# Ordering the last stage of a four-layer graph network by a planned list over pairs of super-tiles, with q k in seven products, and reordering loads and preparations of the graph part

## The chip, the cores and the metric

The kernel runs on one core of a Trainium2 chip. The metric is the device time of one execution in microseconds (us). Engines are named as in the profile: PE is TensorE (matrix products and transposes), DVE is VectorE, ACT is ScalarE, POOL is GpSimd, SP is SyncE, which here only issues DMAs. Each engine works through its own queue in program order; an instruction that waits for another engine holds up everything behind it in its queue.

## The reference, cut to what matters

The input x is 128 graphs of 64 nodes with 256 features (8192 rows in float32); adj is one 64 x 64 matrix for all graphs. Four layers follow one another, each of the form x = x + layer(relu(layernorm(x))):

```python
# layer 0: two graph convolutions, then four LSTMs over windows of 1..4 nodes
h = relu(einsum('ts,bsh->bth', adj, h @ Wg0 + bg0))
h = relu(einsum('ts,bsh->bth', adj, h @ Wg1 + bg1))
# layer 1: graph product, 256 -> 512 -> 256, batchnorm after each product
# layer 2: diagonal, upper and lower part of adj, each with its own weights
h = einsum('bjf,kfo->kbjo', x, W)
out = adj_0 h[0] + adj_1 h[1] + adj_2 h[2] + bias
# layer 3: causal attention inside each graph, adj added to the scores
q, k, v = split(x @ Wqkv, 3)
scores = where(causal, einsum('btd,bsd->bts', q, k) * scale + adj_mask, NEG)
y = einsum('bts,bsd->btd', softmax(scores), v) @ Wo
```

## The kernel before

The 8192 rows are cut into 16 super-tiles of 512 rows, each four tiles of 128 rows (q = 0 to 3, two graphs in each); the 256 features are two halves of 128 (c = 0, 1). Everything is float32. The program has five parts: the graph part (the two convolutions), the LSTM part, the first product of layer 1, its second product, and the last stage with layers 2 and 3. PSUM has 8 banks that `bank()` hands out in turn, so a bank is used again eight requests later.

**How the order is set.** The order of the instructions on every engine is the order in which the program makes them; no scheduler moves them. In most parts the program first fills a list `events` with `at(t, fn, ...)`, where t is a planned time, sorts it by t and calls the functions. The planned times set nothing but the order. A "round" of the graph part is 10 planned us, one super-tile in each of its steps.

**Graph part (lines 288 to 475).** `load` (L298) brings x of a super-tile by one DMA (four for the first); `stats`, `root`, `shift` and `relu` make the layernorm: bn_stats and bn_aggr on DVE, an add on DVE and the power -1/2 on POOL (L316), a small product on DVE (L319), the relu on ACT (L323). PE multiplies with adj (`aggregate0`, L331) and with Wg0 (`weigh`, L341), DVE adds the row sums of adj times the bias (L347), ACT makes the relu (L352). The product with Wg1 (L370) has the seven-product form of a 2 x 2 block product: POOL makes sums of blocks (`sums`, L362), PE adds seven 128 x 256 products into three banks a, b and c, and DVE reads a bank between two products that are added into it (`begun`, L377, and `add`, L384). The last super-tile takes the direct form (L391). Among the rounds stand preparations for later parts: `adjacencies` (L139, DVE), `degrees_root` (L154, POOL), `degrees`, `normalize` (L176) and sums of the first LSTM weights (`weight_sum`, L275, POOL). Wg0 is loaded from ACT's queue (L104).

**Second product (L795 to L881).** The list form with seven products; at its end come the batchnorm coefficients co2 (L881), then transposes of Wqkv (L890) and the weight product Wq Wk^T into wqk (L897, L899).

**Last stage (L904 to L1010).** `rest(s)` is a generator for one super-tile, and `pipelined(..., 2)` starts one every second step and lets each live one take one step in turn, the youngest first. The steps are: load x1 and affine of the batchnorm on DVE (L912); transposes back to rows (L227) and add (L228); layernorm (L191 to L195, L201), then the bias bl2 added on POOL as one 128 x 1024 operation (L922); products with the three parts of adj, 64 rows at a time (L933), copied to `ag` half by ACT and half by DVE (L938); the product with the three weights (L946) and add (L948), layernorm; transposes (L957, L958); q k as eight direct 128 x 512 passes (L964) copied by ACT (L966), and the values times Wv Wo (L972, L974); scores (L980), mask and maximum (L983, L986), exponentials with their sums on ACT (L988); transposes of these (L993, L995); the product with the values (L1001), the division and the sum (L1004), and the store.

Of the kernel before, what the change touches and what calls it, by code (L numbers as in the profile page):

```python
# [20 lines left out]
def kernel(ctx: ExitStack, tc: tile.TileContext, a: dict, out: bass.AP):  # L21
# [82 lines left out]
    wg0 = weight("wg0", a["Wg0"], first, nc.scalar)  # L104
# [34 lines left out]
    def adjacencies():  # L139

        nc.vector.tensor_add(lbias, con["bih"], con["bhh"])


        scr = first.tile([P, P], F32, tag="scr", name="scr")
        nc.vector.tensor_add(scr, adj_bd, ident)
        nc.vector.reduce_sum(deg[:, 0:1], scr, axis=AX.X)
        nc.vector.tensor_mul(scr, scr, ident)
        nc.vector.reduce_sum(deg[:, 1:2], scr, axis=AX.X)
        nc.vector.tensor_add(ahT, adjT_bd, ident)
        nc.vector.reduce_sum(deg[:, 2:3], ahT, axis=AX.X)  # L150
        nc.vector.tensor_add(deg[:, 0:1], deg[:, 0:1], deg[:, 2:3])
        nc.vector.tensor_sub(deg[:, 0:1], deg[:, 0:1], deg[:, 1:2])
# [136 lines left out]
    with tc.tile_pool(name="pa", bufs=2) as pa, tc.tile_pool(name="pax", bufs=3) as pax:  # L289
        events, wih0, made = [], [], []  # L290

        def graph_part(s):
# [5 lines left out]
            def load():  # L298
                v["xt"] = pax.tile([P, Q, D], F32, tag="xt", name="xt")
                for part in ([slice(q, q + 1) for q in range(Q)] if s == 0 else [slice(0, Q)]):  # L300
                    nc.sync.dma_start(v["xt"][:, part, :], x_r[s, :, part, :])
# [35 lines left out]
            def weigh(k):  # L337
                p_ = v["W", k] = bank().rearrange("p (q d) -> p q d", q=2)
                for q in range(2):
                    for c in range(KC):  # L340
                        nc.tensor.matmul(p_[:, q, :], v["g0"][:, c, ts(2 * k + q, P)], wg0[:, c, :],  # L341
# [62 lines left out]
            if s == 0:  # L404
                halves = ((slice(0, 2), -8.6), (slice(2, 4), -7.4))
# [30 lines left out]
            for k in range(4):  # L436
                at(late + 7.2 + 0.7 * k, sums, k)
# [21 lines left out]
            if s == 4:  # L459
                at(5.0, adjacencies)  # L460
                at(11.5, degrees_root)
                at(13.3, lambda: made.append(degrees()))
            if s == 5:
                at(0, lambda: wih0.append(load_lstm(a["WihT"][0], "wih", lwa)))
            if s == 7:
                at(0.4, lambda: normalize(made[0]))
            if s == 9:
                for k in range(4):
                    at(0.4 + 2.5 * k, lambda k=k: weight_sum(wih0[0], k))
# [298 lines left out]
    with tc.tile_pool(name="pz", bufs=1, reuse_waits="tile") as pz:  # L768
# [19 lines left out]
        wqk = late.tile([P, KC, D], F32, tag="wqk", name="wqk")  # L788
        wvo = late.tile([P, KC, D], F32, tag="wvo", name="wvo")
# [111 lines left out]
        weight_product(0, wT[:, KC : 2 * KC, :], wqk)  # L901


    with tc.tile_pool(name="pc", bufs=2, reuse_waits="tile") as pc, \  # L904
            tc.tile_pool(name="pc1", bufs=1, reuse_waits="tile") as pc1:

        def rest(s):
            x1 = pc.tile([P, Q, D], F32, tag="x1", name="x1")
            nc.sync.dma_start(x1, x1d[s])
            y = [yslot(s, c) for c in range(KC)]  # L910
            for c in range(KC):
                nc.vector.tensor_scalar(y[c], y[c], co2[:, 0, c : c + 1], co2[:, 1, c : c + 1],  # L912
                                        op0=ALU.mult, op1=ALU.add)
            yield
            x2 = pc.tile([P, Q, D], F32, tag="x2", name="x2")
            to_token_major(lambda c, q: y[c][:, ts(q, P)], x1, x2)
            if s == 0:
                weight_product(2, wo, wvo)


            h = layernorm_relu(pc, x2)
            nc.gpsimd.tensor_add(x2, x2, bcast_q(bl2))  # L922
            yield
            ag = pc1.tile([P, KC, 3, SUP], F32, tag="ag3", name="ag3")

            for c in range(KC):
                for q2 in range(0, Q, 2):
                    half = [bank()[:, : 6 * T].rearrange("p (q k n) -> p q k n", q=2, k=3)
                            for _ in range(2)]
                    for q in range(2):  # L930
                        for b in range(2):
                            r = slice(b * T, (b + 1) * T)
                            nc.tensor.matmul(half[b][:, q], h[r, q2 + q, ts(c, P)], adj3[r, :, r],  # L933
                                             start=True, stop=True)
                    for b in range(2):
                        copy = nc.vector.tensor_copy if b else nc.scalar.copy
                        to = ag[:, c, :, q2 * P : (q2 + 2) * P].rearrange("p k (q n) -> p q k n", q=2)
                        copy(to[:, :, :, b * T : (b + 1) * T], half[b])  # L938
            yield
            x3 = pc.tile([P, Q, D], F32, tag="x3", name="x3", bufs=4)  # L940
            for q2 in range(0, Q, 2):
                p_ = bank().rearrange("p (q d) -> p q d", q=2)
                for q in range(2):
                    for n in range(3 * KC):
                        c, k = divmod(n, 3)
                        nc.tensor.matmul(p_[:, q, :], ag[:, c, k, ts(q2 + q, P)], wl2[k][:, c, :],  # L946
                                         start=(n == 0), stop=(n == 3 * KC - 1))
                nc.vector.tensor_add(x3[:, q2 : q2 + 2, :], x2[:, q2 : q2 + 2, :], p_)  # L948


            h = layernorm_relu(pc, x3, "ln_h3")
            yield
            h3T = pc.tile([P, KC, SUP], F32, tag="h3T", name="h3T")
            for c in range(KC):
                p_ = bank()
                for q in range(Q):
                    nc.tensor.transpose(p_[:, ts(q, P)], h[:, q, ts(c, P)], ident)  # L957
                nc.vector.tensor_copy(h3T[:, c, :], p_)  # L958
            yield
            qk = pc1.tile([P, KC, SUP], F32, tag="qk", name="qk")  # L960
            for o in range(KC):
                p_ = bank()
                for c in range(KC):
                    nc.tensor.matmul(p_, wqk[:, c, ts(o, P)], h3T[:, c, :],  # L964
                                     start=(c == 0), stop=(c == KC - 1))
                nc.scalar.copy(qk[:, o, :], p_)  # L966
            hw = pc.tile([P, Q, D], F32, tag="hw", name="hw")
            for q2 in range(0, Q, 2):
                p_ = bank().rearrange("p (q d) -> p q d", q=2)
                for q in range(2):  # L970
                    for c in range(KC):
                        nc.tensor.matmul(p_[:, q, :], h3T[:, c, ts(q2 + q, P)], wvo[:, c, :],  # L972
                                         start=(c == 0), stop=(c == KC - 1))
                nc.scalar.copy(hw[:, q2 : q2 + 2, :], p_)  # L974
            yield

            p_ = bank()
            for q in range(Q):
                for c in range(KC):
                    nc.tensor.matmul(p_[:, ts(q, P)], qk[:, c, ts(q, P)], h3T[:, c, ts(q, P)],  # L980
                                     start=(c == 0), stop=(c == KC - 1))
            sc = pc1.tile([P, Q, P], F32, tag="sc", name="sc")
            nc.vector.scalar_tensor_tensor(sc, p_.rearrange("p (q n) -> p q n", q=Q), D ** -0.5,  # L983
                                           bcast_q(smask), op0=ALU.mult, op1=ALU.add)
            mx = pc.tile([P, 3, Q], F32, tag="mx", name="mx", bufs=3)
            nc.vector.tensor_reduce(mx[:, 0, :], sc, AX.X, ALU.max, negate=True)  # L986
            for q in range(Q):
# [61 lines left out]
```

## Time and profile before

| what | value |
|---|---|
| median of 3 runs (lowest, highest) | 1912.3 us (1910.62, 1914.24) |
| the profiled execution | 1910.58 us, its span 1908.7 us |
| busy share of PE, DVE, ACT, POOL | 98%, 57%, 46%, 31% |
| graph part | up to about 181 us |
| LSTM part, first and second product | up to 1470 us |
| last stage | 1470 to 1908.7 us |
| last stage, share of L946 (PE) in the chain of waits from 1400 us on | 32.6% |

The span is the time from the first to the last recorded instruction of the profiled execution; the difference to its time lies around it. In the chain of waits each piece has a start, a length, and the engine and line that the end of the program waited for in that piece. PE records two passes for one product in float32 (x8 for four products). In a line on waits the first number is the total, the second the count and the third the longest. In a timeline each line has the start, the length, the engine, the line of the kernel, the operation with its result and operands, and in brackets how long the engine had been idle and what released it.

### The profile page before, as it was taken

The page shows a single profiled execution, that of the slowest core. Times are in us where ns is not written, and L with a number is a line of the kernel's source. Part 1 is how long each engine was busy: PE and PEld are TensorE (multiplying, and loading weights), DVE is VectorE, ACT ScalarE, POOL GpSimd, SP SyncE. Part 2 cuts the span into 40 slices and gives each one's busy share as a digit, 9 for nine tenths or more (in the row PEclk, how much of TensorE's full clock was granted, in tenths as well). Part 3 has the DMA queues.
Part 4 walks back from the last instruction along what each step waited for, and adds up shares of the span by engine and source line. Part 5 has one row for each costly group of instructions (what it writes and reads, how often), then busy time and mean ns, then how long its engine had stood idle before and what let it go on. Part 6 is the DMA issues. An engine that isn't in the chain of part 4 may idle for free.

```text
span 1908.7 us, 19347 instructions
## 1 busy us (share of the span) xinstructions
PE 1874.8 (98%) x7022; PEld 1160.6 (61%) x7022; DVE 1092.3 (57%) x2155; ACT 882.2 (46%) x1509; POOL 598.9 (31%) x434
## 2 busy tenths in 40 slices
PE   7999999999999999999999999999999899999998
PEld 7897444444445666665444444555444788888886
DVE  6775777635446345445633334688786555565554
ACT  6676666534435335434533333444574333333332
POOL 4341412543325433331522224533152211111110
PEclk9999999999999999999999999999999999999999
DMA  4110001000001000000000001233100001111111
GB/s 138 56 56 1 1 1 32 13 1 0 1 0 44 1 0 1 1 0 23 0 0 1 1 0 44 77 111 111 64 1 30 26 23 45 45 45 34 33 34 45
DMA packets 49471, 54.31 MB, mean 28 GB/s; under 512 B 3040, under 2 KB 44768, under 8 KB 49376
## 3 DMA queue, kind: packets, MB, share of 16 engines
q1 hardware_dynamic: 48640, 52.61, 8.8%
q8 instruction: 56, 0.92, 0.2%
q10 hardware_dynamic: 736, 0.46, 0.1%
q14 instruction: 39, 0.32, 0.1%
HBM read 36.28 MB, written 16.78 MB: 28 GB/s over the span
## 4 chain that ended last, share of the span: by engine, by line
PE 94%; DVE 3%; ACT 1%; POOL 1%; issue 1%; DMA 0%; SPq 0%; DVEq 0%; ACTq 0%; POOLq 0%
PE ps L599 34%; PE ps L605 19%; PE ps L946 9%; PE ps L515 6%; PE ps L834 5%; PE ps L972 3%; PE ps L964 3%; PE ps L331 3%; PE ps L341 2%; PE ps L933 2%; PE ps L370 2%; PE ps L980 1%; PE ps L217 1%; PE ps L1001 1%; PE ps L227 1%; PE ps L957 1%
## 5 line engine op out<-in xcount | busy, mean ns | idle before, releaser
L621 DVE TENSOR_TENSOR gate<-gate,ps 128x512 f32<-128x512 f32 (+2 forms) x378 | 223.9, 619 | 446.2 <-PE ps L605 366.9
L599 PE MATMUL ps<-tx,wih 128*128 128x512 f32 (+2 forms) x1008 | 446.8, 542 | 2.7 <-ACT gate L624 1.0
L599 PE MATMUL ps<-hT,wih 128*128 128x512 f32 (+2 forms) x756 | 338.5, 541 | 0.0
L624 ACT COPY gate<-ps 128x512 f32<-128x512 f32 (+2 forms) x252 | 134.5, 534 | 378.2 <-PE ps L605 325.1
L599 PEld LDWEIGHTS ps<-tx,wih 128*128 128x128 f32 x1008 | 190.5, 190 | 193.0 <-issue 130.8
L617 ACT ACTIVATE gate<-gate,lbias 128x512 f32<-128x512 f32 (+2 forms) x252 | 216.7, 860 | 157.8 <-DVE gate L621 157.8
L605 PE MATMUL ps<-h,whh 128*128 128x512 f32 (+2 forms) x576 | 256.6, 527 | 0.0
L599 PEld LDWEIGHTS ps<-hT,wih 128*128 128x128 f32 x756 | 143.6, 190 | 141.6 <-issue 79.6
L605 PE MATMUL ps<-th,whh 128*128 128x512 f32 (+2 forms) x432 | 192.4, 527 | 0.0
L194 POOL TENSOR_TENSOR ln_rn<-ln_rn,mhalf 128x4 f32<-128x4 f32 x48 | 48.6, 1012 | 389.1 <-DVE ln_rn L193 389.1
L605 PEld LDWEIGHTS ps<-h,whh 128*128 128x128 f32 x576 | 109.4, 190 | 100.2 <-issue 76.5
L946 PE MATMUL ps<-wl,ag 128*128 128x256 f32 x768 | 168.4, 379 | 0.0
L644 POOL TENSOR_TENSOR gate<-gate 128x1024 f32<-128x1024 f32 (+2 forms) x36 | 71.9, 2017 | 304.7 <-ACT gate L617 304.7
L201 ACT ACTIVATE ln_h<-x,ln_rn 128x256 f32<-128x256 f32 x128 | 66.5, 589 | 199.1 <-DVE ln_rn L195 199.1
L946 PEld LDWEIGHTS ps<-wl,ag 128*128 128x128 f32 x768 | 144.8, 190 | 19.1
L644 POOL TENSOR_TENSOR cell<-gate 128x1024 f32<-128x1024 f32 (+2 forms) x36 | 79.4, 2226 | 175.2 <-ACT gate L617 175.2
L605 PEld LDWEIGHTS ps<-th,whh 128*128 128x128 f32 x432 | 82.1, 190 | 75.2 <-issue 57.4
L515 PE MATMUL ps<-ag,w 128*128 128x512 f32 x256 | 112.3, 592 | 0.0
L644 POOL TENSOR_TENSOR cell<-gate,cell 128x1024 f32<-128x1024 f32 (+2 forms) x32 | 65.1, 2052 | 109.3 <-ACT gate L617 109.3
L624 DVE COPY gate<-ps 128x512 f32<-128x512 f32 (+2 forms) x126 | 78.5, 623 | 20.9 <-PE ps L605 20.9
L649 ACT ACTIVATE gate<-cell 128x1024 f32<-128x1024 f32 (+2 forms) x72 | 68.1, 951 | 29.5 <-POOL cell L644 29.5
L617 ACT ACTIVATE gate<-ps,lbias 128x512 f32<-128x512 f32 (+2 forms) x126 | 79.6, 631 | 3.9 <-PE ps L605 1.0
(199 smaller groups left out, 2693.4 us busy)
## 6 DMA issues: line engine op xcount, KB each, us to landing
xt<-in_x_dram SPq DMA_DIRECT2D x31, 512.0 KB, 4.6
x1d<-xt SPq DMA_DIRECT2D x16, 512.0 KB, 3.0
x<-x1d SPq DMA_DIRECT2D x16, 512.0 KB, 4.4
out_dram<-x SPq DMA_DIRECT2D x16, 512.0 KB, 3.2
wih<-in_WihT_dram SPq DMA_DIRECT2D x16, 256.0 KB, 4.5
whh<-in_WhhT_dram SPq DMA_DIRECT2D x12, 256.0 KB, 5.1
wl<-in_W_dram SPq DMA_DIRECT2D x3, 256.0 KB, 2.9
wqkv<-in_Wqkv_dram SPq DMA_DIRECT2D x1, 768.0 KB, 6.2
```

Source lines behind the costliest of these rows:

```text
L201: nc.scalar.activation(h[:, q, :], src[:, q, :], AF.Relu, bias=rn[:, 1, q : q + 1], scale=rn[:, 0, q : q + 1])
L331: nc.tensor.matmul(p_[:, ts(q, P)], v[h][:, q, ts(c, P)], adjT_bd, start=True, stop=True)
L515: nc.tensor.matmul(p_, con["w1"][:, c, ts(o, P)], ag[:, c, :], start=(c == 0), stop=(c == KC - 1))
L599: nc.tensor.matmul(wide(p_[:, :N]), wih[0][:, OF[k], gi, :], x_, start=first_, stop=(j == 0), skip_group_check=True)
L605: nc.tensor.matmul(p_[:, :N], whh[0][:, OF[k], gi, :], h_, start=False, stop=True, skip_group_check=True)
L617: nc.scalar.activation(to, r[bank_][:, :N] if bank_ else to, fn, bias=lbias[:, l, m : m + 1])
L621: nc.vector.tensor_add(slot(n, hc), slot(n, hc), r[bank_][:, :N])
L624: op(slot(n, hc), r[bank_][:, :N])
L644: fn(*((t["G"] if isinstance(t, dict) and "G" in t else st["c"])[:, n, :, : st["N"]] for t in tiles))
L649: nc.scalar.activation(o_, c, AF.Tanh)
L834: nc.tensor.matmul(banks[name], w2[:, OF[j], k, :], x_, start=(new and k == 0), stop=(k == 1), skip_group_check=True)
L946: nc.tensor.matmul(p_[:, q, :], ag[:, c, k, ts(q2 + q, P)], wl2[k][:, c, :], start=(n == 0), stop=(n == 3 * KC - 1))
```

## The change

**Last stage.** The generator and its turns are gone. `rest(s, at, ...)` now fills one list for all super-tiles, with planned times given per pair of super-tiles (an even and the next odd one), 52.5 planned us from pair to pair, and special times for the first and last pair. Each step of before becomes one or more functions. New in what is computed: q k of 15 super-tiles in seven products with 128 x 256 blocks (`qsum` on DVE, `qproduct`, `qcopy` on ACT, `qadd` on DVE), the last one direct (`qdirect`); the sums of weight blocks for it, `aqk`, are made on POOL from wqk (four copies, four sums) right after the weight product; the bias is added in four 128 x 256 pieces (`biased`); the first super-tile's layernorm is made in two halves; x2 has three buffers and ag two. In the last super-tile exps are turned, and results stored, in halves.

**Graph part.** Wg0 is loaded on SP's queue behind x of the first super-tile; x of the second super-tile comes in four DMAs, not one; the root of the first half-layernorm comes earlier; `sums` 2 and 3 move ahead of the power (8.1) on POOL; `adjacencies` is cut into four pieces in four rounds, with the steps that need it three rounds later; `normalize` moves to round 9; the sums of the first LSTM weights stand 1.6 instead of 2.5 planned us apart.

The diff, cut:

```diff
-    wg0 = weight("wg0", a["Wg0"], first, nc.scalar)
...
-                for part in ([slice(q, q + 1) for q in range(Q)] if s == 0 else [slice(0, Q)]):
+                for part in ([slice(q, q + 1) for q in range(Q)] if s < 2 else [slice(0, Q)]):
...
+                at(-20, lambda: con.update(wg0=weight("wg0", a["Wg0"], first)))
+            if s == 0:
-                halves = ((slice(0, 2), -8.6), (slice(2, 4), -7.4))
+                halves = ((slice(0, 2), -9.1), (slice(2, 4), -7.4))
...
-                at(late + 7.2 + 0.7 * k, sums, k)
+                at(late + (7.2, 7.9, 8.0, 8.05)[k], sums, k)
...
-                at(5.0, adjacencies)
-                at(11.5, degrees_root)
-                at(13.3, lambda: made.append(degrees()))
+                pieces = adjacencies()
+                for k in range(4):
+                    at(5.0 + ROUND * k, next, pieces, None)
+                at(11.5 + ROUND * 3, degrees_root)
+                at(13.3 + ROUND * 3, lambda: made.append(degrees()))
...
-            if s == 7:
-                at(0.4, lambda: normalize(made[0]))
+            if s == 9:
+                at(5.0, lambda: normalize(made[0]))
             if s == 9:
                 for k in range(4):
-                    at(0.4 + 2.5 * k, lambda k=k: weight_sum(wih0[0], k))
+                    at(0.6 + 1.6 * k, lambda k=k: weight_sum(wih0[0], k))
...
         weight_product(0, wT[:, KC : 2 * KC, :], wqk)
+        for o in range(2):
+            for c in range(2):
+                nc.gpsimd.tensor_copy(aqk[:, 2 * o + c, :], wqk[:, c, ts(o, P)])
+        weight_sums(aqk)
+    PERIOD, HALF = 52.5, SUP // 2
...
+        def rest(s, at, only_pair, t_T, t_n, t_G, t_W, t_h, t_QH, t_S, t_soft, t_E, t_O, end):
...
+            def biased(q):
+                nc.gpsimd.tensor_add(v["x2"][:, q, :], v["x2"][:, q, :], bl2)
...
+            def qsum(k):
+                if k == 1:
+                    v["t"] = pc1.tile([P, 5, HALF], F32, tag="tq", name="tq")
+                t = v["t"]
+                nc.vector.tensor_sub(t[:, k], *(None, (b_(0, 1), b_(0, 0)), (b_(1, 1), t[:, 1]),
+                                                (b_(1, 1), b_(0, 1)), (b_(1, 0), t[:, 2]))[k])
...
+                nc.tensor.matmul(v["q", name], aqk[:, OF[j], :], x_, start=new,
+                                 stop=(name, j) in (("a", 4), ("b", 3), ("c", 2)), skip_group_check=True)
+            def qcopy(o, n, name):
+                nc.scalar.copy(c_(o, n), v["q", name])
+            def qadd(o, n, name):
+                nc.vector.tensor_add(c_(o, n), c_(o, n), v["q", name])
...
+            at(t_T - 8, load)
+            for c in range(KC):
+                at(t_T - (2 if first_ else 9) + 0.6 * c, affine, c)
+            for k in range(2):
+                at(t_T + 0.1 * k, turn, k)
+                at(t_T + 0.1 * k + 0.01, turned, k)
+            if first_:
+                norm("x2", "h2", True, (t_T + 0.455, t_T + 1.8), (t_T + 3.2, t_T + 4.6))
+                for q in range(Q):
+                    at(t_T + 7 + 0.7 * q, biased, q)
+            else:
+                norm("x2", "h2", False, (t_n, t_n + 1.2), (t_n + (11.9 if s % 2 and s > 1 else 4.1),))
+                for q in range(Q):
+                    at(t_n + (14.5 if s % 2 else 10.5) + 0.7 * q, biased, q)
+            for k in range(4):
+                at(t_G + 0.8 * k, graphs3, *((k % 2, k // 2) if first_ else (k // 2, k % 2)))
+            for k in range(2):
+                for q in range(2):
+                    at(t_W[k] + 2.6 * q, weigh, k, q)
+                at(t_W[k] + 5.3, weighed, k)
+            norm("x3", "h3", False, (t_W[0] + 5.8, t_W[1] + 5.8), (t_W[1] + 8.8,))
+            for c in range(KC):
+                at(t_h + 0.04 * c, h3, c)
+                at(t_h + 0.45 * (c + 1), h3_copy, c)
+            if not end:
+                for k in range(1, 5):
+                    at(t_h + 1.1 + 0.35 * k, qsum, k)
+                u = 0.43
+                for k, (name, j) in ((0, ("c", 2)), (1, ("a", 1)), (4, ("b", 5)), (5, ("a", 6)),
+                                     (8, ("b", 3)), (9, ("a", 7)), (13, ("a", 4))):
+                    at(t_QH + k * u, qproduct, name, j)
+                for q, k in enumerate((2, 6, 10, 14)):
+                    at(t_QH + k * u, hv, q)
+                at(t_QH + 2 * u, qcopy, 0, 0, "a")
+                at(t_QH + 3 * u, qadd, 0, 0, "c")
+                at(t_QH + 5.1 * u, qcopy, 1, 1, "b")
+                at(t_QH + 6.1 * u, qcopy, 0, 1, "a")
+                at(t_QH + 8 * u, hv_copy, 0)
...
+            at(t_S, scores)
+            at(t_S + 2, masked)
+            at(t_soft, largest)
             for q in range(Q):
+                at(t_soft + 0.7 + 0.6 * q, exps, q)
...
+            rest(2 * i, at, i, -8.6 if first_ else -40.2, -38.3, 0, (7.0, 12.6), 29.0, 32.6, 40.0, 42.7,
+                 46.3 if end else 46.5, 50.4 if end else 48.85, False)
+            if first_:
+                at(-7.6, weight_product, 2, wo, wvo)
+            rest(2 * i + 1, at, i, -3.0 if first_ else -27.6, 1.5 if first_ else -25.4, 12.3 if first_ else 3.5, (17.8, 26.5), 39.1,
+                 (42.0, 45.4, 48.7, 49.6, 52.1) if end else 42.0, 46.7 if end else 50.6,
+                 49.5 if end else 59.5, 53.0 if end else 64.7, 53.8 if end else 75.6, end)
```

The functions that are not shown (`turn`, `turned`, `graphs3`, `weigh`, `weighed`, `h3`, `h3_copy`, `hv`, `scores`, `masked`, `largest`, `exps`, `turn_e`, `turned_e`, `attend`, `attended`) hold the instructions of the former steps.

## The prediction

> **What bounds the kernel now.** I read the engines' busy time first, then the chain of waits of the last stage, then TensorE's waits stage by stage, then the timelines around each wait.
>
> ```profile
> span 1908.7 us, 19347 instructions
> PE 1874.8 (98%) x7022; PEld 1160.6 (61%) x7022; DVE 1092.3 (57%) x2155; ACT 882.2 (46%) x1509; POOL 598.9 (31%) x434
> ```
>
> TensorE (PE) is the bound everywhere; the other engines matter only where PE waits for them. The chain of the last stage shows one super-tile after another without a gap:
>
> ```profile
> 1554.34 0.87 PE ps L227 x8
> 1555.21 10.36 PE ps L946 x48
> 1565.57 3.43 PE ps L964 x8
> 1569.00 3.45 PE ps L972 x16
> 1572.46 0.44 PE ps L993 x4
> 1572.89 2.80 PE ps L933 x32
> 1575.69 1.02 PE ps L957 x8
> 1576.72 1.79 PE ps L980 x16
> 1578.51 1.73 PE ps L1001 x8
> 1580.23 0.87 PE ps L227 x8
> ```
>
> A super-tile is 25.89 us (1554.34 to 1580.23) of pure PE work, a pair 51.8. So here time is saved by less PE work, or by less idle time at the stage's two ends; and any wait that the new order brings into the middle is lost in full. PE's waits in this stage stand at its head and tail:
>
> ```profile
> PE ps L933 <- ACT ln_h L201: 3.5, 1, 3.5
> PE ps L957 <- DVE ag L938: 3.2, 1, 3.2
> PE ps L1001 <- DVE eT L995: 0.8, 1, 0.8
> ```
>
> In the graph part a round is 10.05 us of PE work; PE waits 6.9 us for its first input, 1.8 for wg0, 1.3 for L352, and twice for L384. A quiet round:
>
> ```profile
> 86.49 1.01 POOL L316 TENSOR_TENSOR ln_rn<-ln_rn,mhalf 128x4 f32<-128x4 f32 x1 [0.22 <-DVE ln_rn L315]
> 87.47 0.73 POOL L362 TENSOR_TENSOR t<-g 128x256 f32<-128x256 f32 x1
> 87.53 0.68 DVE L319 SCALAR_TENSOR_TENSOR ln_rn<-ln_mv,ln_rn 128x4 f32<-128x4 f32 x1 [0.40 <-POOL ln_rn L316]
> 89.31 0.42 DVE L384 TENSOR_TENSOR h<-h,ps 128x256 f32<-128x256 f32 x1
> 89.65 1.03 PE L370 MATMUL ps<-t,wg 128*128 128x256 f32 x4
> ```
>
> Two things to see. The power on POOL is followed on DVE by shift (L319), an add from PSUM (L347), L377 and L384; the second product of the last line (a6, at 90.08) overwrites the bank that L384 reads, and L384 ends at 89.73, 0.35 us earlier. Where PE did wait for it, it started 0.14 us after L384's end (59.50 to 59.64), so the true slack is 0.21. And L319, 0.16 us elsewhere, takes 0.68: it ends with the POOL subtraction beside it. DVE operations with two SBUF inputs and POOL operations exclude each other, and take turns:
>
> ```profile
> 308.01 1.75 DVE L561 TENSOR_TENSOR tx<-hT 128x512 f32<-128x512 f32 x1
> 1414.84 1.34 DVE L820 TENSOR_TENSOR T<-hT,T 128x512 f32<-128x512 f32 x1
> 1415.59 1.72 POOL L822 TENSOR_TENSOR z<-z 128x512 f32<-128x512 f32 x1
> ```
>
> Alone these are 0.68 on DVE and 1.27 on POOL. Operations that read PSUM (L347, 0.68 beside POOL) and bn_stats are not held up.
>
> **The change, part by part: last stage.**
>
> *Seven products.* q k is eight 128x512 passes now, 3.43 us; seven products of 128x256 at 0.43 (L370, 0.86 for two) are 3.01. 15 super-tiles save 0.42: **-6.3**. The new subtractions and adds go to DVE and ACT (57% and 46% busy). After the 64-row graph products the transposes of h3 take 1.02 instead of 0.87; now these products stand together once per pair: **-1.2**.
>
> *Head.* From the second product's end (1470.13) to 1503.9 are 33.8 us with 22.4 of PE work (weight transposes 1.3, weight products 3.44, 2 x 0.87, 2 x 2.80, 10.36): 11.4 idle. New: DVE makes the affine of super-tile 1 before that of 0 (4 x 0.5), taking turns with the POOL copies of aqk (0.25 each), so y of super-tile 0 is whole at 1476.7, not 1475.1. The eight added POOL operations are done at 1478.8, before the first power is due (1480.0): hidden; without that cover at most 0.8. Halves in the layernorm give relus from 1481.3 to 1483.4, and PE's graph products end at 1484.6 with the transposes of super-tile 1 already done: 9.3 of work in 14.5, 5.2 idle, and about 0.8 where super-tile 1's first graph products wait for its relus. **-5.4**. The old 3.2 us wait of L957 goes, because 5.2 us of weigh and other work lie between.
>
> *Tail.* From the last scores (1896.33) to the end are 12.4 us with 3.9 of work (0.44 + 2 x 1.73). New order: three hv (2.58), attend of 14 (1.73), then transposes and attend of 15. They cover mask, maximum and exps (0.2 + 0.6 + 0.8 + 1.6), PE waits about 0.5 for eT, ends 7.0 after the scores, and DVE and the last, half as large, DMA take 4.6 more: 11.6 with 6.5 of work. But the transposes of 14's exps come 0.9 late: on ACT the copy of qdirect 1 stands ahead of three exps. **-2.5**.
>
> *The middle, where nothing waits today.* I sorted the new list and laid each engine's operations one after another, from the end of the odd super-tile's second weigh (0). PE: attend of the former odd one, two turns, weigh, h3T of the even one at 5.2, weigh until 8.65, its products and hv, odd h3T at 15.1. DVE in its order: weighed 0.6, stats and attended 2.75, turned 1.2, four stats 2.15, two h3 copies 1.2, four qsums 1.5 (128x256, half of 0.68 and overhead): only then weighed, at 9.5 instead of 8.8. Two stats, root, power, shift end at 12.85; four relus at 0.52 with an hv copy among them end at 15.6. The last transposes of h3 want them at 15.4: PE waits **0.3**.
>
> Then: h3 copies end at 17.2, and qsums follow. On POOL the bias pieces of the next odd super-tile (128x256: 0.73, as L362) start as its relus end: 16.6, 17.65, then back to back. Each qsum takes its turn with a piece: they end at 20.5, not 18.6. Behind them on DVE are mask and maximum (0.6 + 0.7), then on ACT exps 0 and 1 (0.78 after the maximum's start, 0.39 each), and only then the copy of bank b, for which product b3 waits: it starts at 23.1, PE is there at 21.5. **1.6**. Product a7 waits 0.3 more, behind exp 2 and a copy. In all 2.24 per pair, in the seven pairs that have a successor: **+15.7**. Bounds: without turns the subtractions end at 18.6 and 0.7 is left (+5); if every piece went first and DVE came 1 us later, 3.5 (+24). I take 2.24: lock and order both stand in rows.
>
> Sum of the stage: -6.3 - 1.2 - 5.4 - 2.5 + 15.7 = **+0.3**.
>
> **Graph part.** *sums at 7.2, 7.9, 8.0, 8.05*: all four POOL subtractions now precede the power (8.1). It starts 1.12 later (87.61, after two at 0.69, instead of 86.49); L319 is then free of the lock and saves 0.51; 0.61 late with 0.21 slack makes **0.40** per round, over some 12 rounds **+4.8**. Below, it costs 0 if DVE's adds make up time; above, 1.1 - 0.2 = 0.9 a round (+11) if the lock wait stays. I take 0.40.
>
> *adjacencies in pieces*: the two stalls on L384 end with 59.64 and 111.07, where PE's next turn was due at 57.77 and 110.18. The first, 1.9, is the burst of adjacency work: gone, since pieces of 0.2 to 1.5 delay root by less than the 1.2 by which the power now comes later anyway. **-1.9**; if that cover went, up to +0.8 for the largest piece. *Weight sums of wih* (four of 1.27 on POOL) fit between power and next sums: -0.9; but the first starts right at the power's end and holds L319 1.2, degrees_root 0.4 in another round: together **+0.7**. *normalize* only moves (PE 0.43).
>
> *wg0 from SP after x*: PE's 1.8 wait goes, ACT is free 0.45 earlier, the root of the first half comes before two stats: first product at 6.5 instead of 6.9. On SP s=1's three more issues (0.4 to 0.7) and wg0 push x of s=2 and wg1p some 2.3 later (wg1p landed 8.4 after its issue at 4.52); POOL's copies of it, and the power of s=2 behind them, come no earlier than now. relu1's second half then lets PE go on at 18.5, not 20.22: **-1.7** (bounds -3.5: both waits and the start gone; +2.3: all waits for the later queue). [...] Here s=0's four quarters of 128 KB landed 2.6 after issue and overlapped, against 4.7 for 512 KB, so I keep the row.
>
> Sum: 4.8 - 1.9 + 0.7 - 1.7 = **+1.9**. Whole: +2.2 on the profiled 1910.6 (span 1908.7 and 1.9 around it), 1912.8. The median of the runs, 1912.3, is 1.7 above the profiled one, so I forecast **1914.5**.
>
> **Rivals.** *Bias pieces and subtractions miss each other* (faster): the pieces start with the relus; if those are 2 us earlier or later against h3T, or the pieces wait for all four relus, b3 waits 0.1: 7 x 1.5 = 10.5 less, **1904**; with the power's lateness covered too, 1899. For it: DVE has idle time at 15 to 16; against: h3T itself waits for the relus, so both stay tied. *VectorE late in the odd half* (slower): weighed, stats, root and shift of the odd super-tile are queued behind 9.4 us of DVE work, and behind its relus wait h3T, scores and all products. It decides once that work exceeds 9.2; each 0.1 more costs 0.7 in all; 1 us (locks on shift, turned waiting for x1) makes **1921.5**. *The products save nothing*: if a 128x256 product cost more than 0.49, the 6.3 would go (1921); L370's rows speak against it.
>
> **How the numbers follow.** Forecast 0.42 (own range 1908 to 1919), pieces missing each other 0.30, VectorE late 0.22, the rest 0.06. The range 1900 to 1923 reaches over both. About 0.2% (3.8 us) is what a measurement can tell from no change. Faster: 0.30, and 0.08 from the forecast's edge and the rest; same 0.24, all from the forecast; slower: 0.22, and 0.16 from the forecast's upper part and the rest.
>
> **What would show it.** Right: PE waits for ACT copies of qk at two products per pair, some 13 us in all; qsums of 0.9 to 1.2 beside bias pieces; L384 as releaser once per round, 0.4 each, with rounds of 10.45; no waits over 2 us at the stage's head. Wrong: pairs of 51 us without waits; rounds still 10.05; PE waiting for relus of h3 by more than 0.5.

## The result and the profile after

The changed kernel takes 1910.52 us (median of 4 runs, 1910.29 to 1910.96), the kernel before on the same chip 1913.27 (4 runs, 1910.62 to 1914.39): ratio 0.9988, 95% interval 0.9971 to 1.0005. The forecast was 1914.5. The profiled execution of the changed kernel took 1910.37 us, span 1908.6, against 1908.7 before: the two spans are equal, though the stretches that were changed are not.

The engines' line on the page of the changed kernel:

```profile
PE 1872.3 (98%) x7112; PEld 1174.0 (62%) x7112; DVE 1142.5 (60%) x2264; ACT 890.0 (47%) x1539; POOL 612.5 (32%) x491
```

PE is busy 2.5 us less, DVE 50 us more. PE's waits in the whole span of the changed kernel (total, count, longest):

```profile
PE ps L1051 <- ACT qk L1055: 7.9, 7, 1.1
...
PE ps L372 <- DVE h L386: 4.1, 12, 1.3
PE ps L947 <- DVE hS L938: 1.8, 1, 1.8
PE ps L999 <- ACT h L974: 1.6, 1, 1.6
```

The two waits of over 3 us at the head of the last stage are gone (1.8 and 1.6 stand there now). Two new ones have come, and both recur: once in each of seven pairs PE waits for ScalarE's copy of q k (L1055), and in twelve rounds of the graph part for DVE's L386 (L384 before). From PE's timeline, the graph products of both super-tiles of a pair, one pair after the other:

```profile
1588.96 5.47 PE L999 MATMUL ps<-adj,h 64*128 64x192 f32 x64
1641.45 5.47 PE L999 MATMUL ps<-adj,h 64*128 64x192 f32 x64
```

A pair takes 52.49 us; before it took 51.78.

| stretch (from PE's timeline) | before | after | difference | predicted |
|---|---|---|---|---|
| start to the first product with Wg1 (c2 of the first super-tile, L370; L372 after) | 25.27 | 23.88 | -1.4 | -1.7 |
| from there to the first LSTM product (177.89; 180.60) | 152.62 | 156.72 | +4.1 | +3.6 |
| LSTM, first and second product | 1292.2 | 1292.2 | 0.0 | 0 |
| last stage (from 1470.1; from 1472.8) | 438.6 | 435.8 | -2.8 | +0.3 |
| of it: seven pairs that have a successor | 7 x 51.78 | 7 x 52.49 | +5.0 | +8.7 |
| of it: the rest (head, tail, last pair) | | | -7.8 | -8.4 |

In names of products such as c2 or a6 the letter is the bank and the number says which of the seven products it is. So a loss of 2.7 us in the graph part and a gain of 2.8 in the last stage cancel. The gain is itself made of about -8 at the ends and +5 in the middle.

### The profile page after: what moved, and what is told of

It reads as the page before. It is cut to its first block, busy times and chain, and to the rows that moved or that the text cites. A ratio compares the mean times of both kernels' runs of the same rounds, so it can differ in the third digit from the quotient of the medians.

```text
span 1908.6 us, 19724 instructions
## 1 busy us (share of the span) xinstructions
PE 1872.3 (98%) x7112; PEld 1174.0 (62%) x7112; DVE 1142.5 (60%) x2264; ACT 890.0 (47%) x1539; POOL 612.5 (32%) x491
## 4 chain that ended last, share of the span: by engine, by line
PE 88%; DVE 6%; POOL 3%; ACT 3%; issue 1%; DMA 0%; ACTq 0%; DVEq 0%; POOLq 0%
PE ps L605 34%; PE ps L611 19%; PE ps L1011 8%; PE ps L521 6%; PE ps L841 5%; PE ps L999 2%; PE ps L1075 2%; PE ps L1051 2%; PE ps L333 2%; PE ps L372 2%; PE ps L219 1%; PE ps L1116 1%; POOL t L364 1%; DVE tq L1038 1%; PE ps L1085 1%; PE ps L229 1%
## 5 line engine op out<-in xcount | busy, mean ns | idle before, releaser
L967 POOL TENSOR_TENSOR ln_rn<-ln_rn,mhalf 128x4 f32<-128x4 f32 (+1 forms) x33 | 32.8, 994 | 311.0 <-DVE ln_rn L966 310.5
L974 ACT ACTIVATE h<-x,ln_rn 128x256 f32<-128x256 f32 x128 | 68.2, 593 | 104.2 <-DVE ln_rn L970 104.2
```

The source lines that it names most:

```text
L974: nc.scalar.activation(v[tag][:, q, :], v[src][:, q, :], AF.Relu, bias=v["rn"][:, 1, q : q + 1], scale=v["rn"][:, 0, q : q + 1])
```

## The experiments

Theory: each of the two recurring waits is an ordering of two queues, and not a price of the seven products. In the pair, GpSimd's bias pieces slow the subtractions on VectorE, these hold mask and maximum, these hold the exponentials, and the copy of bank b stands behind two exponentials on ScalarE. In the graph part, four subtractions ahead of the power hold the shift (L321), and L386 stands behind it. Rivals: the copy cannot be made in the time of two products whatever stands ahead; the longer round comes from another reordering; the loss in the graph part and the gain in the last stage are scatter of the two profiles.

| run | time, us (runs) | ratio to before on the same chip | 95% interval | pair, us |
|---|---|---|---|---|
| bias_dve | 1902.68 (4) | 0.9947 | 0.9932 to 0.9962 | 51.02 |
| copies_first | 1900.94 (4) | 0.9939 | 0.9925 to 0.9954 | 50.87 |
| direct | 1904.89 (4) | 0.9958 | 0.9942 to 0.9975 | 51.49 |
| sums_back | 1904.57 (4) | 0.9958 | 0.9943 to 0.9973 | 52.49 |
| graph_only | 1915.27 (10) | 1.0018 | 1.0008 to 1.0027 | (old order) |
| last_only | 1907.17 (10) | 0.9980 | 0.9970 to 0.9989 | 52.49 |
| both_orders | 1893.26 (4) | 0.9903 | 0.9886 to 0.9920 | 50.87 |
| tail_swap | 1892.53 (4) | 0.9900 | 0.9885 to 0.9915 | 50.87 |
| filled | 1917.86 (6) | 1.0033 | 1.0020 to 1.0045 | (old order) |
| filled4 | 1909.79 (11) | 0.9989 | 0.9980 to 0.9998 | (old order) |

**bias_dve: the bias pieces leave the subtractions alone**

```diff
-                    at(t_n + (14.5 if s % 2 else 10.5) + 0.7 * q, biased, q)
+                    at(t_n + (20.5 if s % 2 else 10.5) + 0.7 * q, biased, q)
-                nc.gpsimd.tensor_add(v["x2"][:, q, :], v["x2"][:, q, :], bl2)
+                (nc.vector if s % 2 and s > 1 else nc.gpsimd).tensor_add(v["x2"][:, q, :], v["x2"][:, q, :], bl2)
```

> The changed kernel with one edit: the four bias pieces of the odd super-tiles (1, 2 and 16 excepted where they already stand elsewhere) go from GpSimd, where the end of the relus releases them beside the four subtractions of the even super-tile, to VectorE behind the copy of the turned exponentials, five places further down the plan. Theory (the subtractions are slow because GpSimd works beside them, and the late subtractions hold the mask, the exponentials and so ScalarE's copy of bank b): the two slow subtractions fall from 0.94 to 0.42 us, the wait of PE for copies of q k at L1055 falls from 1.13 us in a pair to under 0.2, a pair takes 51.1 to 51.4 us instead of 52.49, and the span is 1899 to 1901 instead of 1908.6 (7 x 1.1 to 1.35). Rival (the copy stands late on ScalarE because two exponentials are ahead of it, whatever VectorE does): the subtractions become short, the wait stays over 0.7 us and the pair over 52.0, span 1905 to 1909. Second rival (four more 0.42 us instructions on VectorE late in the pair hold the attention's adds): the pair is 52.5 or longer.

First the timeline of one pair in the changed kernel, all engines, around the wait:

```profile
1681.16 2.55 POOL L987 TENSOR_TENSOR x<-x,bl 128x256 f32<-128x256 f32 x3 [0.24 <-ACT h L974]
...
1682.19 0.94 DVE L1038 TENSOR_TENSOR tq<-h3T 128x256 f32<-128x256 f32 x1
...
1683.06 0.94 DVE L1038 TENSOR_TENSOR tq<-h3T,tq 128x256 f32<-128x256 f32 x1
...
1685.36 0.40 ACT L1098 ACTIVATE sc<-sc,mx 128x128 f32<-128x128 f32 x1 [2.07 <-DVE mx L1095]
...
1686.14 0.35 ACT L1055 COPY qk<-ps 128x256 f32<-128x256 f32 x1
...
1686.55 0.48 PE L1051 MATMUL ps<-h3T,aqk 128*128 128x256 f32 x1 [1.13 <-ACT qk L1055]
```

Read it from the bottom. PE waits for a copy of 0.35 us. ScalarE made that copy at 1686.14 although it had been idle for 2.07 us until 1685.36: the instruction at the head of its queue was an exponential, and that waited for the maximum on DVE. DVE was late because its last two subtractions took 0.94 us each beside the bias pieces (0.85 each, 2.55 for three). The same place in bias_dve:

```profile
1679.30 0.42 DVE L1038 TENSOR_TENSOR tq<-h3T,tq 128x256 f32<-128x256 f32 x1
...
1681.86 0.35 ACT L1055 COPY qk<-ps 128x256 f32<-128x256 f32 x1
...
1682.45 0.38 PE L1051 MATMUL ps<-h3T,aqk 128*128 128x256 f32 x1
```

The subtraction takes 0.42 us, the copy ends 0.24 us before PE starts the product, and the bracket is gone. The pair falls by 1.47 us to 51.02, a little under the range (51.1 to 51.4), and the span to 1899.8. The rival that the order on ScalarE alone makes the wait (over 0.7 left) falls in this form: with VectorE on time the two exponentials ahead of the copy cost product b3 nothing, and a7 and what follows it about 0.15 us.

**copies_first: the copies leave the exponentials**

```diff
-                at(t_soft + 0.7 + 0.6 * q, exps, q)
+                late = s % 2 == 0 and only_pair < NP - 1
+                at(t_soft + (1.93 + 0.2 * q if late else 0.7 + 0.6 * q), exps, q)
```

> The changed kernel with one edit: in the pairs 1 to 7 the four exponentials of the even super-tile stand on ScalarE behind the copies of banks b and a of the odd super-tile, not around them. Theory (queue order: the copy waits behind two exponentials that VectorE releases late): the wait of PE for copies of q k falls from 1.13 us to under 0.2 a pair although the subtractions stay at 0.94 us, and the turned exponentials become late by 0.3 to 0.8; a pair takes 51.4 to 52.0 us, span 1901.5 to 1905. Rival (the copy itself cannot be done in the time of two products, whatever stands ahead): the wait stays over 0.7 us, pair 52.5 to 53. Second rival (the exponentials are what PE then waits for): wait for the turned exponentials over 1 us, pair 52.5 or more.

In copies_first the subtractions are as slow as before, and it no longer matters:

```profile
1680.25 0.95 DVE L1038 TENSOR_TENSOR tq<-h3T,tq 128x256 f32<-128x256 f32 x1
...
1681.35 0.80 ACT L1055 COPY qk<-ps 128x256 f32<-128x256 f32 x2 [0.87 <-PE ps L1051]
...
1682.45 0.59 PE L1051 MATMUL ps<-h3T,aqk 128*128 128x256 f32 x2
```

Now the copies wait for PE (0.87), not PE for the copies. The pair takes 50.87 us, better than its range of 51.4 to 52.0, since the exponentials, which I had expected 0.3 to 0.8 late, are not: the last one starts at 1683.72 with 0.38, and the transposes that turn them start at 1684.17 without a wait. So there are two ways to cut one chain: subtractions slowed beside GpSimd and exponentials ahead of the copy (order) are both needed for the wait. The stronger cure is the order, by 0.15 us a pair.

**direct: q k of all super-tiles in four full products**

```diff
-            if not end:
+            if not isinstance(t_QH, tuple):
+                for o in range(KC):
+                    at(t_QH + 1.7 * o, qdirect, o)
+                ...
+            elif not end:
```

> The changed kernel with q k of all super-tiles as four full products in two banks, as the last two have them, and the plan otherwise kept; no subtractions, no aligned adds. Theory (the seven products save what their count says, 15 x 0.42 us, and their waits in the middle take it back, 0.5 to 1.5 us a pair): PE's time of a pair rises by 0.84 and the waits for copies of q k (1.13) and for the seventh product (0.22) go, so a pair takes 51.9 to 52.2 us instead of 52.49, span 1904 to 1907. Rival (the waits belong to the order of the list, not to the seven products): the pair takes 53.0 to 53.4 us, span 1912 to 1915. Second rival (the seven products save nothing): a pair of 51.2 or less.

The pair takes 51.49, lower than expected (51.9 to 52.2). With no products of seven, the q k and hv block of a super-tile lasts 6.89 us on PE's timeline; in copies_first it lasts 6.47. The predicted saving of 0.42 per super-tile is there. Against copies_first a pair gains 0.62, not 0.84: with the seven products PE reaches the odd super-tile's h3 transposes 0.2 too early for its relus (1.08 instead of 0.87). In the order of the changed kernel the seven products therefore cost 1.00 us a pair net (52.49 against 51.49), though they save 0.62 where the copies stand in time.

**sums_back: the power between the graph part's subtractions again**

```diff
-                at(late + (7.2, 7.9, 8.0, 8.05)[k], sums, k)
+                at(late + 7.2 + 0.7 * k, sums, k)
```

> The changed kernel with one edit: in the graph part the four subtractions stand at 7.2, 7.9, 8.6 and 9.3 of the round again, so that the power of the next norm comes between them on GpSimd. Theory (four subtractions ahead of the power make VectorE wait for the power in each round, 0.40 to 0.44 us): a steady round takes 10.05 us instead of 10.49, the waits of 12 rounds go, the LSTM starts near 175.5 instead of 180.60 and the span is 1903 to 1904.5. Rival (the longer round comes from another reordering, the spread preparation or the loads): rounds stay over 10.35, the LSTM starts after 179.

A round of the changed kernel, all engines:

```profile
86.34 0.74 POOL L364 TENSOR_TENSOR t<-g,t 128x256 f32<-128x256 f32 x1
...
87.03 1.02 POOL L318 TENSOR_TENSOR ln_rn<-ln_rn,mhalf 128x4 f32<-128x4 f32 x1
...
88.08 0.17 DVE L321 SCALAR_TENSOR_TENSOR ln_rn<-ln_mv,ln_rn 128x4 f32<-128x4 f32 x1 [1.04 <-POOL ln_rn L318]
...
89.91 0.45 PE L372 MATMUL ps<-t,wg 128*128 128x256 f32 x1 [0.21 <-DVE h L386]
```

and of sums_back:

```profile
94.47 1.02 POOL L318 TENSOR_TENSOR ln_rn<-ln_rn,mhalf 128x4 f32<-128x4 f32 x1 [0.22 <-DVE ln_rn L317]
...
95.52 0.68 DVE L321 SCALAR_TENSOR_TENSOR ln_rn<-ln_mv,ln_rn 128x4 f32<-128x4 f32 x1 [0.41 <-POOL ln_rn L318]
...
97.63 1.03 PE L372 MATMUL ps<-t,wg 128*128 128x256 f32 x4
```

In the first, the power begins as soon as the last subtraction ends; DVE idles 1.04 us in front of the shift, and PE's a6 waits for L386, so that b5 and a6 no longer stand together. The bracket shows only half of the loss: the round is 10.49 us against 10.05. In the second, the shift is held by the subtraction beside it (0.68 instead of 0.17), and PE still finds its bank free. From the first product with Wg1 to the LSTM the stretch is 150.14 us against 156.72, 6.6 less; the span is 1903.0. The rival (another reordering) falls.

**graph_only and last_only: one half of the change each**

These two put the changed graph part before the old last stage, and the old graph part before the changed last stage; no other line differs.

> The kernel before with the graph part of the changed one and its own last stage. Theory (the two halves of the change add, and nothing passes from one to the other): the LSTM starts at 180.6 to 182.0 us as in the runs of the changed kernel (177.89 before), the last stage takes 438.6 us from the last second product as before, span 1911.4 to 1912.8. Rival (the last stage's length differs by a few us from run to run with the clock, and the 2.9 us between the two profiles are such a difference): the last stage takes 435.5 to 437.5 here, span 1908.5 to 1910.5.

> The kernel before with the last stage of the changed one and its own graph part. Theory (the halves add): the LSTM starts at 177.9 us, the last stage takes 435.7 us, a pair 52.49, span 1905.5 to 1906.2. Rival (the last stage's gain is the profiles' scatter): the last stage takes 437.5 us or more, span 1907.5 to 1909.

The two halves have opposite signs, both beyond the uncertainty: 1.0018 and 0.9980. In the trace of graph_only the LSTM starts at 180.61 as expected and the span is 1913.1, 0.3 above the expected range; its last stage takes 440.2 us, 1.6 more than before, with the same waits but with a granted clock of 0.62 and 0.82 in 1504 to 1516, where it was 1.00 in the kernel before. So the rival was right that the old last stage's length varies, and wrong in the direction. In last_only the last stage takes 435.2 (expected 435.7) and the pair 52.49, but the span is 1907.0, 0.8 above the expected range, since its LSTM starts at 179.54, 1.65 later than in the kernel before with the same code: there the clock granted to PE in 20 to 30 us was 0.83 instead of 1.00. So the halves add, within a scatter of 1 to 2 us between single profiles, which differ in the clock as said.

**both_orders and tail_swap: what the experiments point to**

both_orders joins sums_back and copies_first. tail_swap adds one edit at the end:

```diff
-                 46.3 if end else 46.5, 50.4 if end else 48.85, False)
+                 46.75 if end else 46.5, 50.4 if end else 48.85, False)
```

> The changed kernel with two of the edits tried before together: the graph part's subtractions at 7.2, 7.9, 8.6 and 9.3 of the round, and the even super-tile's exponentials behind the copies of banks b and a of the odd one. Theory (the two stages do not touch): LSTM at 175.1, a pair of 50.87 us, the sum of both differences, span 1892.5 to 1894. Rival (an earlier start of the later stages meets other transfers or a lower clock): span over 1895.

> As the kernel with both orders, and at the end the turned exponentials of super-tile 14 stand behind the scores of super-tile 15 on PE, not ahead of them. In the changed kernel they took 1.47 us instead of 0.60 since the exponentials come behind a copy of q k. Theory (PE waits there, and everything behind it to the last store moves with it): 0.8 to 1.1 us less than the kernel with both orders, of the last scores to the end 11.4 to 11.8 instead of 11.2, since the transposes now lie in that stretch. Rival (the end is set by the softmax of super-tile 15 and its two half stores, whatever PE does before): less than 0.3 us less.

both_orders takes 1893.26 us, 0.9903 of before: the stages do not touch. Its span of 1891.4 is 1.1 under the expected range; its first product with Wg1 starts at 23.88 as in the changed kernel, and not at 24.94 as in sums_back. In the changed kernel the transposes of super-tile 14's exponentials lie on PE's timeline ahead of the last scores and are stretched by their wait; in tail_swap they follow the scores:

```profile
1894.12 1.47 PE L1106 MATMUL ps<-ident,sc 128*128 128x128 f32 x4
```

```profile
1878.60 1.95 PE L1085 MATMUL ps<-h3T,qk 128*128 128x128 f32 x16
1880.38 0.60 PE L1106 MATMUL ps<-ident,sc 128*128 128x128 f32 x4
```

From the start of the last direct q k products to the start of the last attention products are 11.74 us instead of 12.61 in both_orders. The median falls by 0.7 us, a little under the expected 0.8 to 1.1, and less than the two medians' own uncertainty; what shows the gain is the timeline of the tail. (The span of tail_swap's profile, 1892.3, is 0.9 longer than that of both_orders: its first product with Wg1 starts 1.2 later, and at the head of its last stage the transposes and the weight product behind the first longer gap took 2.15 and 2.90 us, which are 1.44 and 1.89 in both_orders.) tail_swap is faster than both the kernel before and the changed one.

**filled and filled4: PE kept busy in the old head**

```diff
                 weight_product(2, wo, wvo)
+                filler(4)
+        def filler(n):
+            p_ = bank()
+            for _ in range(n):
+                nc.tensor.matmul(p_, wqkv[:, 0, :P], wqkv[:, 0, P : P + 512], start=True, stop=True)
```

(filled has 8 of them here and 7 more ahead of super-tile 0's h3 transposes.)

> The kernel before with PE kept busy in the two long gaps at the start of its last stage: eight full products of 0.43 us into a bank that nobody reads ahead of super-tile 0's graph products (gap 3.47 us), seven ahead of its h3 transposes (gap 3.22). Nothing else changes. Theory (the granted clock falls after PE has stood idle for some us, 0.66 in 1480 to 1485 in the kernel before, 0.54 and 0.78 in 1505 to 1515 in the run with the changed graph part, and this makes part of the scatter of the kernel before, 1909.66 to 1915.30, and part of what the new head gains): the clock is 1.00 from 1475 to 1535, the 32 graph products of super-tile 0 take 3.2 us instead of 4.55, the last stage from the last second product 437.2 us instead of 438.6, the median 1.0 to 2.5 us under that of before, highest minus lowest under 3.5. Rival (the clock falls whatever PE does, or the gaps do not matter to it): the clock shows a stretch under 0.9 in 1475 to 1535 again, the last stage takes 438.4 or more, the median lies within 0.8 us of before.

filled was badly sized: a full product is 0.86 us (recorded as two of 0.43), not 0.43, so 7 us went into a gap of 3.5, and the second set waited itself 3.1 us for a bank that the copies of L938 had not released. It takes 1917.86 us. Its clock is still worth reading: 1.00 behind the first gap, which was filled, and 0.66 in 1505 to 1510 behind the second, where the fillers came 3.1 us late.

> The kernel before with four full products (0.86 us each, as the run with eight showed) into a bank that nobody reads, in the gap of 3.47 us ahead of super-tile 0's graph products alone. Theory (the granted clock falls behind an idle PE, so a filled gap keeps it): 1.00 in 1475 to 1500 and super-tile 0's graph products at their time of 2.87 us, not 4.55; the weights behind them begin 16.63 us after the last second product in the kernel before, here 14.9 to 15.2; the second gap of 3.2 us stays and the clock may fall behind it as before; median 0.5 to 1.7 us under that of before. Rival (the fall does not depend on the gap, or the fillers delay the graph products by what they save): graph products over 3.5 us or the weights 16.4 us or more after the last second product, median within 0.4 us of before.

Busy time and granted clock by stretch (each line: start and end, PE, PEld, DVE, ACT, POOL, clock, DMA share, GB/s). The kernel before:

```profile
1480.00:1485.00 5.00, 3.66 (x24) 3.61 (x26) 2.19 (x5) 3.03 (x6) 2.62 (x2) 0.66 0.00 0
...
1500.00:1505.00 5.00, 1.66 (x15) 1.38 (x14) 3.70 (x10) 3.19 (x8) 1.02 (x1) 1.00 0.00 0
```

filled4:

```profile
1480.00:1485.00 5.00, 4.96 (x37) 2.96 (x35) 2.60 (x6) 3.37 (x7) 2.61 (x2) 1.00 0.04 15
...
1500.00:1505.00 5.00, 2.42 (x12) 2.12 (x13) 3.95 (x9) 3.56 (x8) 0.86 (x1) 0.78 0.00 0
```

With the gap filled the clock stays at 1.00 there, and the weights begin 15.47 us after the last second product instead of 16.63. That is 1.2 of the 1.4 to 1.7 expected: the fillers do not delay the graph products (11.23 us after the last second product, 11.22 before), but these took 3.38 us, not 2.87, for a reason that stays open. The median is 1.9 us under that of before (0.9980 to 0.9998), just outside the expected range. So work that nobody uses made the kernel faster, by 0.1%, and the interval only just excludes no change. Behind the second gap, left open, the clock fell to 0.78 in this run, and in the run of before it did not. So one gap of 3.22 us was followed by 1.00 and another of 3.22 by 0.78, and the length of the gap alone does not say which. A shorter one was enough in other runs: of the eight profiles with the changed last stage, all with a gap of about 1.77 us at its head (and in all of them another of 0.43 some 2 us earlier), the clock fell behind it in last_only to 0.76 and in direct to 0.67, and in tail_swap the transposes and the weight product behind it took 2.15 and 2.90 us (2.21 and 2.82 in direct); in the other five the two took 1.44 and 1.89. What decides between them is not shown. The same 5 us in direct and in the changed kernel, both behind that gap:

```profile
1480.00:1485.00 5.00, 5.00 (x23) 4.38 (x23) 3.79 (x13) 0.59 (x1) 2.45 (x5) 0.67 0.32 103
```

```profile
1480.00:1485.00 5.00, 3.41 (x25) 2.75 (x26) 4.05 (x15) 1.91 (x4) 3.19 (x6) 1.00 0.32 105
```

## Why the prediction was right and wrong

That the time would not change clearly, and the sum by its largest parts, were right; the forecast is 4.0 us too high. Of these, 1.6 lie in the step from the profiled run to the median and 2.4 in the sum: -3.7 in the seven pairs, +0.6 in the rest of the last stage, +0.8 in the graph part. That the result came out as no change was partly luck: the prediction itself gave this 0.24, and 0.38 each to faster and slower, and the median moved down 2.8 us, inside the noise, where it forecast 2.2 up. By its own steps:

- *Seven products, -6.3.* Right: 0.42 per super-tile (direct against copies_first).
- *h3 transposes at 0.87, -1.2.* The right effect, too small: a pair's graph products take 5.40 instead of 2 x 2.80, its h3 transposes 0.87 each when they do not wait, and 0.19 comes back where weights and scores stand beside 64-row products. About -0.3 a pair, not -0.15.
- *Head -5.4, tail -2.5.* With the last pair, predicted -8.4 for all that is not the seven pairs; measured -7.8. The graph products of super-tile 0 end at 1487.1, which is 1484.4 after taking off the later start of 2.7; predicted 1484.6. From the last scores' end to the end are 11.2 us, predicted 11.6. The transposes 0.9 late behind the copy of direct q k 1 were there, 1.47 instead of 0.60, and tail_swap took them away.
- *Middle, +15.7.* Right in its chain of waits, **mis-sized, and this is the term that missed**: 2.24 us a pair predicted, some 1.8 measured. The h3 transposes wait 0.2 (0.3 predicted), b3 is 1.30 late (1.6), a7 and what follows 0.32 (0.3). The step that failed is "Each qsum takes its turn with a piece": the first subtraction still ran alone (0.42) and the others took 0.83, 0.94 and 0.94, so that the four end 3.0 us after they start, not 3.3, and b3 waits 0.3 less; the chain behind them was as priced. That the two engines exclude each other is the prediction's reading of its rows; what the trace shows here is that each of the three longer subtractions ends 0.28 to 0.29 us after one of the bias pieces beside it (pieces from 1681.16, 1681.95 and 1682.81, of 0.82, 0.90 and 0.90 us). Net of the saving, a pair came out at +0.71 instead of +1.24, 3.7 us less over seven pairs.
- *sums before power, +0.40 a round.* Right: 10.49 against 10.45. With the shift held by the weight sums (1.22 long, as predicted), sums_back gives 6.6 us for both, predicted 4.8 + 1.2.
- *Adjacency stall -1.9, and the weight sums' -0.9 and +0.4.* Together -2.4 predicted; from the first product with Wg1 to the LSTM sums_back is 2.5 below before. None of these was run alone, so only their sum is shown.
- *wg0 from SP and the quarters, -1.7.* The wait for wg0 went and PE went on at 18.82 instead of 20.22 (18.5 predicted), -1.4 in the two profiles. The first product did not come earlier in that run (7.23, against 6.90 before and 6.5 predicted); over the eight profiles with this start of the graph part it stands between 6.5 and 7.4, and the first product with Wg1 starts between 23.88 and 26.27; over the four with the old start it stands between 24.75 and 27.10, 1.1 later in the mean. So the gain is there, but 23.88 is the lowest of eight, the term is uncertain by a microsecond, and the three edits in it were not run apart.
- *Median 1.7 above the profiled run.* This failed: the changed kernel's median is 0.15 above its profiled run. The offset was scatter of the old kernel, 1909.66 to 1915.30 in 19 runs on one chip, not a constant. filled4 points to one source of it, the clock behind the old head's gaps (1.00 behind the first one when it is filled, 0.66 before, and a median 1.9 us lower); the changed head has shorter gaps (1.77 and 1.59 us instead of 3.47 and 3.22) and its four runs lie within 0.7 us (last_only's ten within 2.3, filled4's eleven within 3.4). That the smaller scatter comes from the gaps alone is not shown.

The rivals: "pieces and subtractions miss each other" was priced at 1904 for the changed kernel; made to happen in bias_dve, it took 1.47 us off a pair (1.5 priced), which confirms the price and not the case. That the time, 1902.7, lies near 1904 is luck as well: the changed kernel lay 4.0 us under its forecast, and bias_dve took 7.8 off its median, not 10.5. VectorE was not late in the odd half: h3 waited 0.2. The rows of the last part of the prediction came as said (waits at L1051 and L386, slowed subtractions, rounds of 10.45), only smaller in the pair: 7.9 us shown as waits, at one product per pair and not two, and 7 x 1.62 by PE's timeline.

## What to carry to other kernels

When a list is planned by hand, check per engine queue what the head of the queue waits for: a short copy that feeds the bound engine must not stand behind an instruction with a longer chain, and here moving four exponentials behind two copies was worth 9 us of 1910. A change of many parts with no net effect is worth halving before it is dropped: both halves were beyond their uncertainty with opposite signs, and the losing parts were two orders, each undone in a line or two. The wait that the trace printed between two matmuls was less here than what it cost (0.2 printed for 0.44 of the round, 1.13 for 1.30), so measure the loss by period, not by the sum of waits.

## What was not expected of the hardware

- The clock granted to PE fell behind the gap of 3.47 us in both profiles that have it (0.66 in the kernel before and 0.67 in graph_only, over 5 us), behind the gaps of 3.1 to 3.2 us in three of four (0.54 in graph_only, 0.66 in filled, 0.78 in filled4; 1.00 in the kernel before), and behind the gap of about 1.77 us in two of eight (0.76 in last_only, 0.67 in direct; 1.00 in the changed kernel and sums_back), with products as slow in a third, tail_swap (2.15 and 2.90 us instead of 1.44 and 1.89). Behind the gap of 3.47 us the 32 graph products took 4.55 us at 0.66 and 4.79 at 0.67; in the middle of the stage, at 1.00, they take 2.87. Such stretches of some 5 us go with differences of 1 to 2 us between profiles of one code (the old last stage 438.6 us in the kernel before, 440.2 in graph_only).
- In the changed kernel a VectorE subtraction of 128 x 256 in SBUF took 0.42 us alone and 0.83 to 0.94 beside GpSimd's bias pieces, and a bias piece 0.73 alone and 0.85 beside the subtractions (2.55 for three): 0.41 to 0.52 us more on VectorE, 0.12 on GpSimd.
